# A perceiver layer with experts: the last gathered rows added behind the last pair's hidden products, and one summing operation moved between engines

## The chip, the core and the metric

The kernel runs on one core of a Trainium2 chip. The core has TensorE (PE, matrix products), VectorE (DVE), ScalarE (ACT), GpSimd (POOL) and SyncE (SP, which issues transfers). The metric is the device time of one execution in microseconds; the median of three executions before the change is 1019.1 us (1018.79 to 1021.12).

## What is computed

One layer on 256 tokens of width 512, all in fp32: cross attention (16 query heads, 4 key/value heads of 128, keys from 4096 context rows ahead of the 256 own ones, causal among the own), then a state-space mixer, then a mixture of 32 experts of which every token uses 6. Each part is added to x.

```python
x = x + _L0_xattn_ref(_layernorm(x), ctx_2048, wq, wk, wv, wo, wk_ctx, wv_ctx, ...)
x = x + _L0_attn_ref(_layernorm(x), W_in, conv_w, ..., W_out)      # state-space mixer
x = x + _L0_ffn_ref(_layernorm(x), gate_w, wg, wu, wd, sg, su, sd)
# attention
probs = softmax(q @ k_full.T * scale + mask); out = probs @ v_full
# experts
topk_w, topk_i = top_k(sigmoid(x @ gate_w), 6); topk_w = topk_w / sum(topk_w)
act = silu(x @ wg[e]) * (x @ wu[e])
routed = sum over e of combine[t, e] * (act @ wd[e])
return routed + silu(x @ sg) * (x @ su) @ sd
```

## The kernel before

The 256 tokens are two tiles of 128 (t = 0, 1), the 16 heads four groups g of four. A Python program traces the instructions, and a scheduler of the tile framework then fixes the order of each engine's queue from its own estimate of when things are ready. So the order in a queue is mostly that of the text but not always; `tc.issue_after(ins)` pins what is traced in its block behind `ins` on the same engine (an order, not a wait for the end of `ins`). Tiles come from rings: `pp` has four buffers for exponentials, `ps_sc` three and `ps_o` two banks of PSUM.

**Attention.** It runs in steps s = 0 to 8. Step 0 takes the 256 own keys, steps 1 to 8 take 512 context keys each. `scores` (L554) makes one score block, 128 keys by 512 (four heads times 128 queries), on PE (L559), its exponential on ACT (L562), in step 0 the causal mask of a diagonal block on DVE (L565), and the sum of exponentials in `lacc` on DVE: a copy for the first block of a tile (L568), an add for every other one (L570). `values` (L573) multiplies the exponential with v (L579) two scores later and moves the finished product to `oacc` (L583, L585). A tile's step 0 for one g has one score for t = 0 (its diagonal) and two for t = 1 (the second one diagonal): twelve scores in the order g, t. `lacc` and `oacc` serve before that as room for the queries' rotation (L423 to L426).

Each context step's keys and values are computed by PE beside the attention of the step before, by `fast_steps` (L338): a 2 by 2 block scheme with seven products (p1, p6, p2, p7, p5, p4, p3 in this order) instead of eight. It needs sums of weight blocks. T1, T2, T4 are made early on GpSimd (L323). T3 = b22 - b12 overwrites b12, a block of 128x1024 of the loaded weights `wkv`; GpSimd makes it (L336) behind the last query block's scaling (L450), and p7 is the first to read it. The four sums S1 to S4 of the context's blocks (L348 to L351) are GpSimd's too.

**Experts.** The 32 experts are 16 pairs n (L1321). `gate_up` (L1222) makes one pair's hidden product: PE into `ps_egu`, ACT's silu into `si` (L1231), DVE's product into `hid` (L1233, L1234). For pairs 0 to 12, `down` writes each expert's rows to a memory array `ye`, and each token later gathers its rows from there: `gather` (L1181) is six indirect transfers issued by GpSimd for one token tile (L1187), `add` (L1192) six operations on DVE that add a gathered row times its weight to x (L1194). The last three pairs (13, 14, 15) go another way: `spread_hidden` (L1244) multiplies `hid` with a matrix that puts the experts' rows in token order (PE into `hid_sp` and `rest_sp`, ACT copy at L1252, two DVE copies at L1257, giving `hidS`), and `down_into` (L1259) multiplies by the down weights and accumulates all three pairs in two PSUM banks `total[0]`, `total[1]`, one for each token tile (L1264, three products of 128x512 each, two records apiece in the trace). At the end `finish` (L1354) adds `total` to x on DVE and `store` writes it out.

In the text, round n = 14 reads gate_up(14), add of tile 0, gather of tile 1, turn(15), down_into(13), spread(14); round n = 15 reads gate_up(15), add of tile 1, down_into(14), spread(15); then comes down_into(15).

Of the kernel before, what the change touches and what calls it, by code (L numbers as in the profile page):

```python
# [19 lines left out]
P = 128  # L20
# [26 lines left out]
NE = 32  # L47
# [20 lines left out]
def perceiver_layer(ctx: ExitStack, tc: tile.TileContext, a: dict, out: bass.AP):  # L68
# [65 lines left out]
    def layer(ctx, bounded):  # L134
# [193 lines left out]
        def fast_weights(sums):  # L328
            fw = [wpool.tile([P, KD, 512], FP, tag="w", name=f"fast{i}") for i in range(3)]
            fast["T1"], fast["T2"] = carve(fw[0], T, T)  # L330
            fast["T4"], fast["S1"], fast["S2"] = carve(fw[1], T, (2, 2, P), (2, 2, P))
            fast["S3"], fast["S4"], fast["u3"], fast["u2"] = carve(fw[2], (2, 2, P), (2, 2, P), (2, 256), (2, 256))
            for n, t in zip(("T1", "T2", "T4"), sums):
                S.copy(fast[n], t)
            with tc.issue_after(heads_done[-1]):
                G.tensor_tensor(b12, b22, b12, ALU.subtract)  # L336

        def fast_steps(c, behind=None):  # L338
            ct = ctx_tiles.pop(c)
# [203 lines left out]
        def bounded_attention(beside):  # L543

            pp = pool("pp", 4)
            bq = small.tile([P, 3], FP, tag="bq", name="bq", bufs=1)
            V.tensor_reduce(bq[:, 0:1], qw_bc, AX.X, ALU.max, apply_absolute_value=True)
            V.tensor_reduce(bq[:, 1:2], kw_bc, AX.X, ALU.max, apply_absolute_value=True)
            shift = bq[:, 2:3]
            V.tensor_scalar(shift, bq[:, 0:1], bq[:, 1:2], -float(np.sqrt(HD)), ALU.mult, ALU.mult)  # L550
            V.tensor_scalar(shift, shift, BOUND, None, ALU.add)
            outs = {}

            def scores(s, g, t, n):  # L554

                kT, _, r = kv[s]
                i = keys_of(s, t)[n]
                sc = ps_sc.tile([P, REP * P], FP, tag="sc", name="scT")
                TE.matmul(sc, kT[:, g, i * P:(i + 1) * P], qT[:, t, heads4(g), :].rearrange("p h q -> p (h q)"),  # L559
                          start=True, stop=True)  # L560
                pr = pp.tile([P, REP * P], FP, tag="pr", name="prT")
                S.activation(pr, sc, AF.Exp, bias=shift, scale=SCALE if r is None else r[:, i, g:g + 1])  # L562
                if s == 0 and i == t:
                    p3 = pr.rearrange("p (h q) -> p h q", q=P)
                    V.tensor_tensor(p3, p3, upper.unsqueeze(1).to_broadcast([P, REP, P]), ALU.mult)  # L565
                la = lacc[:, t, g, :]
                if s == 0 and n == 0:
                    V.tensor_copy(la, pr)  # L568
                else:
                    V.tensor_tensor(la, la, pr, ALU.add)  # L570
                return pr

            def values(s, g, t, n, pr):  # L573
                _, v, _ = kv[s]
                keys = keys_of(s, t)
                i, last = keys[n], n == len(keys) - 1
                if n == 0:
                    outs[g, t] = ps_o.tile([P, REP * P], FP, tag="o", name="oT")
                TE.matmul(outs[g, t], v[:, i, g * HD:(g + 1) * HD], pr, start=(n == 0), stop=last)  # L579
                if last:  # L580
                    ov = oacc[:, t, g, :]
                    if s == 0:
                        V.tensor_copy(ov, outs.pop((g, t)))  # L583
                    else:
                        V.tensor_tensor(ov, outs.pop((g, t)), ov, ALU.add)  # L585
                    if s == NC:
                        ps = ps_sc.tile([P, REP * P], FP, tag="sc", name="ps_l")
                        TE.matmul(ps, ones, lacc[:, t, g, :], start=True, stop=True)
                        rl = lacc[:, t, g, :]
                        V.reciprocal(rl, ps)  # L590
                        V.tensor_tensor(aT[:, t, heads4(g), :].rearrange("p h q -> p (h q)"), ov, rl, ALU.mult)

            pending = []
            for s in range(NC + 1):
                if s < NC:
                    steps = [(s, g, t, i) for g in range(NKV) for t in range(NT) for i in range(len(keys_of(s, t)))]
                else:
                    steps = [(s, g, t, i) for t in range(NT) for g in range(NKV) for i in range(len(keys_of(s, t)))]
                    last_weights()
                extra = []  # L600
                if 0 < s < NC:
                    if s + 1 < NC:
                        load_ctx(s + 1)
                    extra = fast_steps(s, heads_done[4] if s == 1 else None)
                    extra.insert(len(extra) // 2, lambda: clear(s - 1))
                done = 0
                for n, st in enumerate(steps):
                    if s == 0 and n == 3:
                        for turn in turns:
                            turn()  # L610
                    pending.append((*st, scores(*st)))
                    if s == 0 and st[3] == len(keys_of(s, st[2])) - 1:
                        q = qT[:, st[2], heads4(st[1]), :]
                        S.activation(q, q, AF.Copy, scale=kw_col)
                    if len(pending) > 2:
                        values(*pending.pop(0))
                    if s < NC:

                        while done < min(len(extra), len(extra) * (n + 1) // (len(steps) - 4)):
                            extra[done]()  # L620
                            done += 1
                    elif n > len(steps) // NT + 1:
                        for f in beside():
                            f()
            for p in pending:
                values(*p)

        def general_attention():
            with ExitStack() as gctx:
# [11 lines left out]
                stats = {}  # L641
                for turn in turns:
                    turn()

                for s in range(NC + 1):
                    if 0 < s < NC:
# [542 lines left out]
                got.append(yk)  # L1189
            return got  # L1190

        def add(got, t):  # L1192
            for k, yk in enumerate(got):
                V.scalar_tensor_tensor(x_sb[:, t, :], yk, m["w8"][:, t, k:k + 1], x_sb[:, t, :], ALU.mult, ALU.add)  # L1194

        class Rounds:


            def __init__(self, ctx, weights):
                pool = lambda name, bufs, **kw: ctx.enter_context(tc.tile_pool(name=name, bufs=bufs, **kw))  # L1200
                self.r, self.weights = 0, weights
                self.e2, self.e4 = pool("e2", 2), pool("e4", 4)
                self.ps_x, self.ps_gu = pool("ps_x", 2, space=PSUM), pool("ps_gu", 2, space=PSUM)
                self.ps_t, self.ps_ye = pool("ps_t", 1, space=PSUM), pool("ps_ye", 3, space=PSUM)
                self.rows, self.xgT, self.hid, self.hidT = {}, {}, {}, {}

            def fetch(self, n):
                for i in range(2):
# [13 lines left out]
            def gate_up(self, n):  # L1222

                hid = self.hid[n] = self.e2.tile([P, 2 * FE], FP, tag="hid", name="hid")
                for i in range(2):
# [5 lines left out]
                    S.activation(si, ps[:, 0:FE], AF.Silu)  # L1231
                    c0 = 2 * P + i * REST
                    V.tensor_tensor(hid[:, i * P:(i + 1) * P], si[:, 0:P], ps[:, FE:FE + P], ALU.mult)  # L1233
                    V.tensor_tensor(hid[:, c0:c0 + REST], si[:, P:FE], ps[:, FE + P:], ALU.mult)  # L1234

            def turn_hidden(self, n):
                tp = self.ps_t.tile([P, 3, P], FP, tag="t", name="hidTp")
# [6 lines left out]
            def spread_hidden(self, n, by):  # L1244
# [9 lines left out]
                    TE.matmul(rest[:, i, :], h[:, 2 * P:3 * P], by[i], start=True, stop=True)  # L1254
                for i in range(2):
                    half = slice(i * REST, (i + 1) * REST)
                    V.tensor_copy(hs[half, 2, :], rest[half, i, :])  # L1257

            def down_into(self, n, total, first, last):  # L1259
                wd = self.weights[3 * n + 2].rearrange("p (j n) -> p j n", j=3)  # L1260
                h = self.hidT.pop(n)
                for t in range(NT):
                    for j in range(3):
                        TE.matmul(total[t], h[:, j, t * P:(t + 1) * P], wd[:, j, :],  # L1264
                                  start=(first and j == 0), stop=(last and j == 2))
# [17 lines left out]
        with ExitStack() as rctx:  # L1283
# [33 lines left out]
                        V.tensor_copy(spread[:, h * (TAIL // 2):(h + 1) * (TAIL // 2), t * P:(t + 1) * P], tp)  # L1317

            FIRST, LAST = HEAD // 2, NP - TAIL // 2
            got, r_y, r_x, r_k = None, (main.e4, "y"), (main.e4, "xg"), (yp, "yk")  # L1320
            for n in range(NP):  # L1321
                main.gate_up(n)
# [2 lines left out]
                if n == LAST + 1:  # L1325
                    add(got, 0)
                    got = gather(ye, row_y, 1, r_y, r_x, r_y, r_x, r_x, r_k)
                if n == LAST + 2:
                    add(got, 1)
                if FIRST <= n + 2 < NP:  # L1330
                    main.fetch(n + 2)
                if FIRST <= n + 1 < NP:
# [3 lines left out]
                elif n > LAST:  # L1336
                    if n == LAST + 1:
                        total = [main.ps_ye.tile([P, DM], FP, tag="ye", name="total") for _ in range(NT)]
                    main.down_into(n - 1, total, n - 1 == LAST, False)
                if n > 0:  # L1340
                    load_piece(3 * (n - 1 + NHELD) + 2)
                if n == FIRST + 1:
# [3 lines left out]
                    got = gather(ye, row_y, 0, r_k, r_y, r_k, r_x, r_k, r_y)  # L1346
                if n < LAST:
                    main.turn_hidden(n)
                else:
                    e0 = 2 * n - (NE - TAIL)  # L1350
                    main.spread_hidden(n, [spread[:, e0 + i, :] for i in range(2)])
            main.down_into(NP - 1, total, False, True)

            def finish(t):  # L1354
# [91 lines left out]
```

## Time and profile before

The profiled execution took 1020.27 us; its span, from the first to the last instruction, is 1018.5 us.

| stretch, us | what runs | PE busy, us | granted clock |
|---|---|---|---|
| 0 to 80 | loads, own queries, keys, values | 74.35 | 1.00 |
| 80 to 100 | step 0 of the attention | 16.79 | 1.00 |
| 100 to 700 | context steps, output projection begun | 599.08 | 1.00 |
| 700 to 850 | mixer, routing | 144.17 | 1.00 |
| 850 to 976 | pairs 0 to 12 | 126.00 | 1.00 |
| 976 to 996 | pairs 13, 14, hidden part of 15 | 20.00 | 1.00 |
| 996 to 1013 | down parts of 14 and 15 | 14.24 | 0.90 |

A line of a group or of the timeline reads: start, length, engine, line of the code, operation, out<-in, shapes, count; in brackets the idle time ahead of it and what ended it. A wait reads: who waited for whom, total, how often, longest. A row of a stretch gives its length, then busy time and count for PE, PEld (weight loads), DVE, ACT, POOL, then the granted clock, the share of the transfer engines and GB/s.

### The profile page before, as it was taken

The numbers are of one execution on the slowest core, as the hardware profiler recorded it, in microseconds if no ns is written. First come the engines' busy times: TensorE is split into PE (matmuls) and PEld (weight loads), VectorE is DVE, ScalarE is ACT, GpSimd is POOL, SyncE is SP. The second block draws the span as 40 slices with busy tenths as digits, with TensorE's granted clock in tenths as the row PEclk, the third lists the DMA queues.
The fourth block names the chain that finished last, engine by engine and source line by source line (L and its number), as shares of the span: only waits on it lengthen the run. The fifth ranks groups of instructions, "written<-read, shape, count | busy, mean of one in ns | idle before, by whom it ended". The sixth has DMA issues, their size and how long they took to land.

```text
span 1018.5 us, 9069 instructions
## 1 busy us (share of the span) xinstructions
PE 994.6 (98%) x2786; PEld 477.5 (47%) x2786; DVE 502.3 (49%) x983; ACT 392.0 (38%) x862; POOL 155.8 (15%) x156
## 2 busy tenths in 40 slices
PE   7998999999999999999999999999999999999996
PEld 3443444444444444444444444444656555555553
DVE  4466555454454454453544544575886662312233
ACT  3644544343443443443444434441446421222210
POOL 5343002001101101101200200000141321000031
PEclk9999999999999999999999999999999999999998
DMA  9725045132222313313304203600364368999732
GB/s 338 214 61 164 2 132 209 32 90 80 57 48 97 82 32 113 84 23 122 82 11 134 64 2 81 165 1 0 102 210 156 115 216 321 355 355 369 272 107 84
DMA packets 136557, 131.94 MB, mean 130 GB/s; under 512 B 80402, under 2 KB 99763, under 8 KB 135347
## 3 DMA queue, kind: packets, MB, share of 16 engines
q1 hardware_dynamic: 129392, 115.71, 35.8%
q0 software_dynamic: 2208, 8.39, 2.4%
q10 hardware_dynamic: 4898, 7.16, 1.9%
q8 instruction: 24, 0.39, 0.1%
q14 instruction: 35, 0.28, 0.1%
HBM read 90.86 MB, written 40.39 MB: 129 GB/s over the span
## 4 chain that ended last, share of the span: by engine, by line
PE 91%; DVE 2%; issue 2%; POOL 1%; DMA 1%; ACT 1%; SPq 0%; DVEq 0%; POOLq 0%; ACTq 0%
PE oT L579 22%; PE scT L559 22%; PE ps_kv L356 16%; PE ps_egu L212 8%; PE ps_self L212 3%; PE ps_ye L1273 2%; PE ps_v L212 2%; PE ps_o L771 2%; PE ps_xbc L212 1%; PE ps_ye L1276 1%; PE ps_k L212 1%; PE ps_out L961 1%; PE xgTp L1218 1%; PE total L1264 1%; PE ps_yd L901 1%
## 5 line engine op out<-in xcount | busy, mean ns | idle before, releaser
L570 DVE TENSOR_TENSOR lacc<-lacc,prT 128x512 f32<-128x512 f32 x260 | 185.4, 714 | 240.7 <-ACT prT L562 239.8
L562 ACT ACTIVATE prT<-scT,bq,rk 128x512 f32<-128x512 f32 x256 | 198.9, 777 | 254.6 <-PE scT L559 242.5
L579 PE MATMUL oT<-prT,v 128*128 128x512 f32 x536 | 272.5, 593 | 4.1 <-DVE prT L565 2.8
L559 PE MATMUL scT<-qT,kT 128*128 128x512 f32 x536 | 270.9, 592 | 0.0
L579 PEld LDWEIGHTS oT<-prT,v 128*128 128x128 f32 x536 | 101.3, 190 | 133.9 <-issue 116.7
L559 PEld LDWEIGHTS scT<-qT,kT 128*128 128x128 f32 x536 | 101.2, 190 | 124.6 <-issue 122.4
L190 POOL TENSOR_TENSOR rk<-pv,mhalf 128x4 f32<-128x4 f32 x32 | 32.3, 1010 | 371.0 <-DVE pv L189 371.0
L1233 DVE TENSOR_TENSOR hid<-si,ps_egu 128x128 f32<-128x128 f32 x32 | 9.2, 287 | 94.2 <-ACT si L1231 94.2
L356 PE MATMUL ps_kv<-wkv,fast 128*128 128x512 f32 x112 | 53.4, 592 | 0.0
L248 ACT ACTIVATE sq<-kraw 128x128 f32<-128x128 f32 x128 | 35.6, 278 | 44.9 <-DVE kraw L374 42.8
L356 PE MATMUL ps_kv<-wkv,ctx 128*128 128x512 f32 x112 | 52.8, 592 | 0.0
L356 PE MATMUL ps_kv<-fast,fast 128*128 128x512 f32 x112 | 52.6, 592 | 0.0
L585 DVE TENSOR_TENSOR oacc<-oT,oacc 128x512 f32<-128x512 f32 x64 | 43.7, 683 | 0.0
L1187 POOL DMA_INDIRECT yk<-ye,row_y x12 | 13.3, 1112 | 139.1 <-DVE hid L1234 135.8
L1279 ACT COPY y_sb<-ps_ye 128x512 f32<-128x512 f32 x26 | 15.2, 586 | 48.8 <-PE ps_ye L1276 43.0
L356 PEld LDWEIGHTS ps_kv<-wkv,fast 128*128 128x128 f32 x112 | 21.3, 190 | 26.8 <-issue 26.8
L356 PEld LDWEIGHTS ps_kv<-wkv,ctx 128*128 128x128 f32 x112 | 21.3, 190 | 26.8 <-issue 23.7
L356 PEld LDWEIGHTS ps_kv<-fast,fast 128*128 128x128 f32 x112 | 21.3, 190 | 26.8 <-issue 21.8
L1231 ACT ACTIVATE si<-ps_egu 128x192 f32<-128x192 f32 x32 | 10.6, 332 | 58.5 <-PE ps_egu L212 56.2
L374 DVE TENSOR_TENSOR kraw<-ps_kv,fast 128x256 f32<-128x256 f32 x42 | 17.8, 424 | 27.9 <-PE ps_kv L356 27.9
L771 PE MATMUL ps_o<-wo,qT 128*128 128x512 f32 x64 | 28.8, 592 | 0.0
L212 PE MATMUL ps_self<-wq,xT 128*128 128x512 f32 x64 | 28.1, 592 | 0.0
(294 smaller groups left out, 1120.6 us busy)
## 6 DMA issues: line engine op xcount, KB each, us to landing
xg<-xn SPq DMA_DIRECT2D x6, 2560.0 KB, 9.3
w_in<-in_pairs_dram SPq DMA_DIRECT2D x14, 768.0 KB, 7.0
ctx<-in_ctxT_dram SPq DMA_DIRECT2D x7, 1024.0 KB, 9.3
kd<-tr SPq DMA_DIRECT2D x112, 64.0 KB, 2.0
kT<-kd SPq DMA_DIRECT2D x28, 256.0 KB, 2.8
xg_sb<-xg SPq DMA_DIRECT2D x28, 256.0 KB, 6.2
ye<-y_sb ACTq DMA_DIRECT2D x26, 256.0 KB, 7.1
wkv<-in_pairs_dram SPq DMA_DIRECT2D x6, 768.0 KB, 7.1
```

Source lines behind the costliest of these rows:

```text
L190: return G.tensor_tensor(dst, v[:, :n], mhalf[:, :n], ALU.pow)
L212: TE.matmul(ps, lhs(k), rhs_of(k), start=(k == 0), stop=(k == KD - 1))
L248: S.activation(sq[:, h, :], raw[:, h, :], AF.Square, accum_out=ss[:, h:h + 1])
L356: TE.matmul(ps, lhs(k), rhs(k), start=(start and k == 0), stop=(k == 1), skip_group_check=True)
L374: V.tensor_tensor(to[n], ps[:, n, :], more[:, n, :], ALU.add)
L559: TE.matmul(sc, kT[:, g, i * P:(i + 1) * P], qT[:, t, heads4(g), :].rearrange("p h q -> p (h q)"), start=True, stop=True)
L562: S.activation(pr, sc, AF.Exp, bias=shift, scale=SCALE if r is None else r[:, i, g:g + 1])
L570: V.tensor_tensor(la, la, pr, ALU.add)
L579: TE.matmul(outs[g, t], v[:, i, g * HD:(g + 1) * HD], pr, start=(n == 0), stop=last)
L585: V.tensor_tensor(ov, outs.pop((g, t)), ov, ALU.add)
L771: TE.matmul(m["ps_o", t], aT[:, t, h, :], wo[j][:, h % 4, :], start=(h == 0), stop=(h == NH - 1))
L1273: TE.matmul(ps[i], h[:, i, :], wd[:, i, :], start=True, stop=False)
```

## The change

Three edits.

- Step 0's sums. For t = 0 the exponential is written straight into `lacc` and masked there, with no copy. For t = 1 the first exponential is kept, and one add of both writes `lacc`. The eight copies at L568 go.
- T3 = b22 - b12 is made by VectorE instead of GpSimd, traced ahead of the ninth score and pinned behind the mask of the seventh.
- The last round. The add of tile 1 leaves its place after gate_up(15). down_into(14) is cut in its two token tiles, and between them stand three of the six adds, spread(15) and the other three adds. The first three are pinned behind the last hidden product of pair 15, the second three behind the last DVE copy of spread(15).

The diff, cut to its core (the new order of round 15 is in its last part):

```diff
-            with tc.issue_after(heads_done[-1]):
-                G.tensor_tensor(b12, b22, b12, ALU.subtract)
+        def last_sum():
+            V.tensor_tensor(b12, b22, b12, ALU.subtract)
...
-                pr = pp.tile([P, REP * P], FP, tag="pr", name="prT")
+                la = lacc[:, t, g, :]
+                alone = s == 0 and t == 0
+                pr = la if alone else pp.tile([P, REP * P], FP, tag="pr", name="prT")
                 S.activation(pr, sc, AF.Exp, bias=shift, scale=SCALE if r is None else r[:, i, g:g + 1])
                 if s == 0 and i == t:
                     p3 = pr.rearrange("p (h q) -> p h q", q=P)
-                    V.tensor_tensor(p3, p3, upper.unsqueeze(1).to_broadcast([P, REP, P]), ALU.mult)
-                la = lacc[:, t, g, :]
-                if s == 0 and n == 0:
-                    V.tensor_copy(la, pr)
+                    masked.append(V.tensor_tensor(p3, p3, upper.unsqueeze(1).to_broadcast([P, REP, P]), ALU.mult).ins)
+                if s == 0:
+                    if n < t:
+                        first_pr.append(pr)
+                    elif not alone:
+                        V.tensor_tensor(la, first_pr.pop(), pr, ALU.add)
                 else:
                     V.tensor_tensor(la, la, pr, ALU.add)
...
+                    if s == 0 and n == 8:
+                        with tc.issue_after(masked[-1]):
+                            last_sum()
...
-        def add(got, t):
-            for k, yk in enumerate(got):
+        def add(got, t, ks=range(TOPK)):
+            for k in ks:
+                yk = got[k]
                 V.scalar_tensor_tensor(x_sb[:, t, :], yk, m["w8"][:, t, k:k + 1], x_sb[:, t, :], ALU.mult, ALU.add)
...
-                    V.tensor_tensor(hid[:, c0:c0 + REST], si[:, P:FE], ps[:, FE + P:], ALU.mult)
+                    self.done[n] = V.tensor_tensor(hid[:, c0:c0 + REST], si[:, P:FE], ps[:, FE + P:], ALU.mult).ins
...
-                    V.tensor_copy(hs[half, 2, :], rest[half, i, :])
+                    self.done[n] = V.tensor_copy(hs[half, 2, :], rest[half, i, :]).ins
...
-            def down_into(self, n, total, first, last):
+            def down_into(self, n, total, first, last, tiles=range(NT)):
...
-                if n == LAST + 2:
-                    add(got, 1)
...
-                    main.down_into(n - 1, total, n - 1 == LAST, False)
+                    if n == NP - 1:
+                        main.down_into(n - 1, total, False, False, [0])
+                        with tc.issue_after(main.done[n]):
+                            add(got, 1, range(0, TOPK // 2))
+                        spread_last(n)
+                        with tc.issue_after(main.done[n]):
+                            add(got, 1, range(TOPK // 2, TOPK))
+                        main.down_into(n - 1, total, False, False, [1])
+                    else:
+                        main.down_into(n - 1, total, n - 1 == LAST, False)
```

Here NP is 16, LAST is 13, and `spread_last(n)` calls `spread_hidden` as the loop did before. The branch for unbounded scores, which isn't taken, calls `last_sum` too.

More of the change, by code (lines that the diff above doesn't have):

```diff
@@ L551, in bounded_attention @@
             V.tensor_scalar(shift, shift, BOUND, None, ALU.add)
-            outs = {}
+            outs, first_pr, masked = {}, [], []
             def scores(s, g, t, n):
@@ L643, in general_attention @@
                     turn()
+                last_sum()
                 for s in range(NC + 1):
@@ L1204, in __init__ @@
                 self.ps_t, self.ps_ye = pool("ps_t", 1, space=PSUM), pool("ps_ye", 3, space=PSUM)
-                self.rows, self.xgT, self.hid, self.hidT = {}, {}, {}, {}
+                self.rows, self.xgT, self.hid, self.hidT, self.done = {}, {}, {}, {}, {}
             def fetch(self, n):
@@ L1256, in spread_hidden @@
                     half = slice(i * REST, (i + 1) * REST)
-                    V.tensor_copy(hs[half, 2, :], rest[half, i, :])
-            def down_into(self, n, total, first, last):
+                    self.done[n] = V.tensor_copy(hs[half, 2, :], rest[half, i, :]).ins
+            def down_into(self, n, total, first, last, tiles=range(NT)):
                 wd = self.weights[3 * n + 2].rearrange("p (j n) -> p j n", j=3)
-                h = self.hidT.pop(n)
-                for t in range(NT):
+                h = self.hidT[n]
+                for t in tiles:
                     for j in range(3):
@@ L1319, in layer, with spread_last @@
             FIRST, LAST = HEAD // 2, NP - TAIL // 2
+            def spread_last(n):
+                e0 = 2 * n - (NE - TAIL)
+                main.spread_hidden(n, [spread[:, e0 + i, :] for i in range(2)])
             got, r_y, r_x, r_k = None, (main.e4, "y"), (main.e4, "xg"), (yp, "yk")
@@ L1348, in layer @@
                     main.turn_hidden(n)
-                else:
-                    e0 = 2 * n - (NE - TAIL)
-                    main.spread_hidden(n, [spread[:, e0 + i, :] for i in range(2)])
+                elif n < NP - 1:
+                    spread_last(n)
             main.down_into(NP - 1, total, False, True)
```

## The prediction

> **What bounds the kernel now.** I read the page's busy times first, then the waits of TensorE (PE), then busy time by stretch, then the timeline of the two stretches where PE is not busy.
>
> ```profile
> PE 994.6 (98%) x2786; PEld 477.5 (47%) x2786; DVE 502.3 (49%) x983; ACT 392.0 (38%) x862; POOL 155.8 (15%) x156
> ...
> PEclk9999999999999999999999999999999999999998
> ```
>
> PE is busy 994.6 of 1018.5 us, so a change that adds or removes no matmul can win only out of the 23.9 us in which PE stands still, and out of the one slice (the last) whose granted clock is below 9 tenths. The waits of PE, with total, count and longest, say which of them the change can touch:
>
> ```profile
> PE oT L579 <- DVE prT L565: 2.8, 2, 1.6
> PE total L1264 <- DVE hidS L1257: 2.6, 1, 2.6
> PE oT L579 <- ACT prT L562: 0.9, 1, 0.9
> PE oT L579 <- DVE oacc L583: 0.4, 1, 0.4
> ```
>
> The stretches, with each engine's busy time and the granted clock:
>
> ```profile
> 80.00:100.00 20.00, 16.79 (x40) 6.63 (x39) 13.26 (x17) 8.76 (x15) 7.64 (x5) 1.00 0.53 159
> 100.00:700.00 600.00, 599.08 (x1397) 264.99 (x1396) 303.57 (x492) 251.50 (x519) 58.69 (x53) 1.00 0.26 75
> ...
> 996.00:1013.00 17.00, 14.24 (x33) 6.32 (x31) 6.89 (x15) 0.92 (x2) 2.58 (x3) 0.90 0.24 76
> ```
>
> Attention is a full PE from 100 to 700 us: what is won before 100 is kept, since PE has nothing to wait for afterwards. PE idles 3.2 us in 80 to 100 and 2.8 us in 996 to 1013, where the clock is also down. Both are places of the diff.
>
> **First step (80 to 100 us).** Number the twelve scores of step 0 as s0 to s11, their value products v0 to v11.
>
> ```profile
> 81.48 0.93 DVE L565 TENSOR_TENSOR prT<-prT,upper 128x512 f32<-128x512 f32 x1 [1.82 <-ACT prT L562]
> 81.82 2.80 POOL L336 TENSOR_TENSOR wkv<-wkv 128x1024 f32<-128x1024 f32 x1
> 82.45 2.46 DVE L568 COPY lacc<-prT 128x512 f32<-128x512 f32 x1
> ...
> 85.46 1.13 DVE L565 TENSOR_TENSOR prT<-prT,upper 128x512 f32<-128x512 f32 x1
> 86.01 1.71 POOL L351 TENSOR_TENSOR fast<-ctx,fast 128x512 f32<-128x512 f32 x1
> 86.51 1.48 DVE L568 COPY lacc<-prT 128x512 f32<-128x512 f32 x1
> ...
> 89.85 1.12 PE L579 MATMUL oT<-prT,v 128*128 128x512 f32 x2 [1.22 <-DVE prT L565]
> ```
>
> A copy at L568 takes 0.43 us alone (its median), yet these two take 2.46 and 1.48 us and end with the GpSimd sums beside them (L336 ends at 84.62, L351 at 87.72). The mask of s3 therefore starts only at 89.12, though its exp ended at 85.6, and v3 waits for it.
>
> Removed: eight copies at L568 (four for query tile 0, whose exp now writes lacc itself; four for tile 1, whose first add takes two tiles). At 0.43 us that is 3.4 us of DVE, as drawn in this trace more, 2.0 + 1.05 us for the two stretched ones. Removed from GpSimd: L336, 2.80 us; its two sums behind it (L350, L351, 1.46 + 1.71 us) move up to about 81.9 to 85.0. Added on DVE: the same subtraction, 128x1024. From rows of two SBUF inputs (0.41 us for 256 columns, 0.69 for 512) I estimate 1.24 us. It is queued behind the mask of s6 (98.40 to 99.09 before), so behind it stand the copy of oT (L583) and the mask of s8. There DVE idled 0.76 and 0.94 us between 99.1 and 102.7 and loses a 0.43 us copy at either end; I take 0. Without that cover it costs 1.24 us once, on v8. Its reader, the product with T3, ran at 122.4, 20 us later.
>
> New DVE line: mask s0 to 82.4, transpose 0.70, mask s2 1.13 (a GpSimd sum still beside it) to 84.3, oT copy 0.68, add 0.69, mask s3 to 86.3. PE line at 0.86 us for each product of two records: v0 82.4, selfT 83.3, s3 83.8, v1, s4, v2 at 86.3, s5 87.2, v3 88.05 (mask ready), v4 88.9, v5 at 89.8 (s5's exp ends about 88.95, its mask 89.7), end 90.6. Before, v5 ended at about 93.06. **Gain 2.4 us.** What comes late next is v6: s6 runs behind two filler products, ended at 97.43, and v6 started at 99.14, waiting for exp (0.69) and mask (0.69). Nothing in the diff shortens this 1.7 us; it moves with the rest.
>
> The rule that speaks against this part stands in the Trainium skill, GPSIMD Engine Reference, section 1 "Specifications": the SBUF interface is shared with VectorE, and not only copies in a two-port mode contend, but also operations with two SBUF inputs. The masks and adds that stay are of that kind, and the two sums now meet them earlier. By the rule alone each of some three such operations could stretch as a copy does (1.0 to 2.0 us), and the gain would be nought. By the row, a mask beside L351 took 1.13 instead of 0.69 us: plus 0.44. I take the row, since it is the same operation beside the same sum; bounds of the head: gain 0 to 4 us (the latter if v6's wait also goes).
>
> **Last pair (976 to the end).** The order on DVE decides here:
>
> ```profile
> 998.93 0.75 DVE L1194 SCALAR_TENSOR_TENSOR x_sb<-yk,lacc,x_sb 128x512 f32<-128x512 f32 x1 [0.57 <-DMA yk<-ye,row_y]
> 999.60 0.85 DVE L1257 COPY hidS<-rest_sp 64x256 f32<-64x256 f32 x2
> ...
> 1001.82 0.75 DVE L1194 SCALAR_TENSOR_TENSOR x_sb<-yk,lacc,x_sb 128x512 f32<-128x512 f32 x1 [0.59 <-DMA yk<-ye,row_y]
> 1002.60 0.29 DVE L1233 TENSOR_TENSOR hid<-si,ps_egu 128x128 f32<-128x128 f32 x1
> ```
> ```profile
> 1002.00:1005.30 3.30, 3.30 (x6) 1.24 (x5) 1.31 (x5) 0.00 (x0) 0.00 (x0) 0.50 0.01 2
> ```
>
> rest_sp of pair 14 was ready at about 991, its copies ran at 999.60 behind ten adds, each waiting for its gathered row; PE stood 2.62 us (997.88 to 1000.50). Pair 15's hid products ran at 1002.60 though the first si was ready at 994.0. After that the clock fell to 0.50 for about 3.4 us (half of it, 1.7 us, lost), and 0.25 us went on pair 15's hidS (L1252, ended 1007.39). Together 4.6 us.
>
> In the change the second tile's six adds stand behind pair 15's hid products, three before and three behind pair 15's hidS copies. The twelve GpSimd gathers stay in place and order (982.48 to 999.2); no queue is moved past, since the SP and ACT queues have no transfer left there but the stores. The gather buffers are held longer, but no later fetch wants them. DVE then: the first tile's last add ends 995.2 (its row's arrival); pair 14's two copies, 0.86, to 996.1; hid products to 997.1 (second si at 996.58); adds 7 to 9, rows there by 997.61, to 999.2; pair 15's copies when rest_sp is done; adds 10 to 12, last row at 1001.82, to 1003.5. PE at 0.43 us a record of 512 columns and 0.215 of 256 (12 in 5.15 us, 4 in 0.86 before): from 996.00 six records of total 0 to 998.57 (pair 14's copies are there at 996.1, needed at 997.7), spread of pair 15, eight records, to 1000.3 (hid there at 997.1), six records of total 1 to 1002.9, which hide hidS (rest copies 1000.5 to 1001.4), twelve of pair 15 to 1008.0. Before, the last record ended at 1012.7. **Gain 4.6 us** (4.7 less 0.1 for waits on semaphores). The adds cost nothing while PE's twelve last records cover them; uncovered, three cost 2.1 us. The stores follow the last product as before.
>
> Here a second rule speaks against: TensorE: Matmul & The Clock Gate, Part 1, gives a window of about 3.4 us of idling before the clock halves, and warns of gaps above some 3 us. This gap is 2.62 us, so read strictly the halving is not the gap's and would stay: gain 2.9. The row says the halving came 1.4 us after that gap and lasted 3.4 us, and that other gaps of 1.7 us left 1.00. I take the row: no gap, no halving.
>
> **Sum.** The profiled execution took 1020.27 us, 1018.5 of span and 1.8 around it. 1020.3 - 2.4 - 4.6 = 1013.3; that execution lies 1.2 above the median of 1019.1, so the median should be 1012.1.
>
> **Rivals.**
> - Both gains as summed: 1012.1. Chance 0.60.
> - The scheduler, planning with a lighter DVE, also puts something between s6 and v6: up to 1.7 us more, 1010.4. For it: q's transpose at 84.83 comes up to 2.4 us sooner and its heads with it. Against: the filler order is set by q's transfer, which is not edited. 0.12.
> - The head gives nothing (masks stretched by the two sums, or PE merely waits longer for v6): 1014.5. 0.14.
> - The tail gives 2.9 (clock halves anyway, or pair 14's copies are queued behind pair 15's hid products): 1013.8. 0.06.
> - Slower: the order of each queue is the scheduler's, not the text's (two products of step 1 ran before s6), and an edit at 80 us makes it plan anew all that follows. If each of the seven context steps got one exposed exp and mask of 1.7 us like v6's, 12 us are lost: 1024. It decides from 1.0 us a step (7.0 in all). Against it: two scores stand between a score and its value product throughout, and PE lost 0.9 us in 600. 0.04.
> - The adds are pulled ahead in another form, or the edges do nothing: about 1017. 0.04.
>
> About 0.3% (3.1 us) is what a measurement of this kernel can tell from no change. Faster by more: 0.91; within: 0.05; slower: 0.04. The range from 1010.0 to 1014.8 leaves out the last two cases and parts of the second and third.
>
> **What would show it.** Right: no wait of total on L1257 and a last slice of PEclk at 9; the last matmul's end about 7 us sooner; no row of L336 or of copies into lacc in step 0; PE's wait for masks before the first ps_kv gone, v6's 1.5 still there. Wrong: a wait of hid_sp on hid, or of total on hidS or yk; a clock of 0.5 without a gap; PE idle between 100 and 700 us.

## The result, and the profile after

The changed kernel took 1013.84 us (median of 5 executions, 1013.70 to 1014.24), the kernel before beside it 1021.08 (1018.79 to 1021.29). The ratio is 0.9938, with a 95% interval of 0.9923 to 0.9952, so about 6.3 us are saved. The profiled execution took 1013.77 us, its span is 1012.0. The kernel before scatters by 2.5 us from one execution to the next, the changed one by 0.5; why is part of the answer below. Two executions of the kernel before on a third chip, of 1517 and 4641 us, are left out of everything that follows.

The page of the changed kernel, its busy times and clock:

```profile
span 1012.0 us, 9057 instructions
...
PE 992.4 (98%) x2786; PEld 477.8 (47%) x2786; DVE 498.6 (49%) x976; ACT 391.7 (39%) x862; POOL 152.6 (15%) x155
...
PEclk9999999999999999999999999999999999999999
```

The number of PE's instructions is the same, its busy time is 2.2 us less although no product was removed: 1.7 us of that is the stretch at half clock, gone from the last slice. ("Half clock" is a granted clock of 0.50 in the rows.) The longest waits of PE:

```profile
PE ps_k L212 <- DMA wkv<-in_wk_ctx_dram: 5.5, 1, 5.5
PE oT L586 <- DVE lacc L570: 1.5, 1, 1.5
PE ps_sh L1064 <- DVE sh L1059: 0.9, 1, 0.9
```

The wait of `total` on the hidS copies is not in the list any more, and of the waits on masks only the one that the prediction left (v6) remains. Busy time by stretch, columns as before:

```profile
80.00:100.00 20.00, 18.47 (x49) 8.02 (x47) 10.49 (x16) 9.93 (x16) 5.41 (x4) 1.00 0.64 199
...
100.00:700.00 600.00, 599.08 (x1397) 265.07 (x1396) 301.88 (x488) 250.66 (x518) 58.66 (x53) 1.00 0.26 74
```

Step 0 on the timeline of the changed kernel (GpSimd's last scaling and its two sums, VectorE's masks and adds, PE's value products):

```profile
81.30 1.04 POOL L452 TENSOR_TENSOR lacc<-lacc,r 128x512 f32<-128x512 f32 x1
82.02 0.87 DVE L570 TENSOR_TENSOR lacc<-lacc,upper 128x512 f32<-128x512 f32 x1 [1.88 <-ACT lacc L567]
82.30 1.73 POOL L352 TENSOR_TENSOR fast<-ctx 128x512 f32<-128x512 f32 x1
...
83.79 0.79 DVE L570 TENSOR_TENSOR prT<-prT,upper 128x512 f32<-128x512 f32 x1 [0.28 <-ACT prT L567]
83.99 1.72 POOL L353 TENSOR_TENSOR fast<-ctx,fast 128x512 f32<-128x512 f32 x1
...
85.10 1.16 DVE L575 TENSOR_TENSOR lacc<-prT 128x512 f32<-128x512 f32 x1
86.18 0.68 DVE L570 TENSOR_TENSOR lacc<-lacc,upper 128x512 f32<-128x512 f32 x1
...
88.64 1.02 PE L586 MATMUL oT<-lacc,v 128*128 128x512 f32 x2
...
97.09 1.22 DVE L338 TENSOR_TENSOR wkv<-wkv 128x1024 f32<-128x1024 f32 x1
97.23 1.12 PE L586 MATMUL oT<-lacc,v 128*128 128x512 f32 x2 [1.51 <-DVE lacc L570]
```

The mask of s3 (86.18) is done long before v3 (88.64), which has no wait in brackets. The subtraction sits behind the mask of s6, takes 1.22 us, and v6 starts beside it. From the first transpose of step 0 on PE (selfT, 79.26 before, 79.75 now) to the second product of context step 1 (117.27 and 115.36) it was 38.01 us and is now 35.61: **2.40 us** saved. The last round on VectorE:

```profile
991.22 0.75 DVE L1206 SCALAR_TENSOR_TENSOR x_sb<-yk,lacc,x_sb 128x512 f32<-128x512 f32 x1 [0.64 <-DMA yk<-ye,row_y]
991.89 0.85 DVE L1269 COPY hidS<-rest_sp 64x256 f32<-64x256 f32 x2
992.77 0.29 DVE L1245 TENSOR_TENSOR hid<-si,ps_egu 128x128 f32<-128x128 f32 x1
...
995.04 2.32 DVE L1206 SCALAR_TENSOR_TENSOR x_sb<-yk,lacc,x_sb 128x512 f32<-128x512 f32 x3
998.60 0.86 DVE L1269 COPY hidS<-rest_sp 64x256 f32<-64x256 f32 x2 [1.24 <-PE rest_sp L1266]
999.48 2.33 DVE L1206 SCALAR_TENSOR_TENSOR x_sb<-yk,lacc,x_sb 128x512 f32<-128x512 f32 x3
```

Each three adds now run in one piece: their rows have come by then, and no add stands ahead of something PE wants. PE has no gap here: six records of `total` at 994.09, the spread at 996.67, six at 998.39, twelve at 1000.97. From pair 13's first `total` product (983.97 before, 982.05 now) to the end of the span it was 34.53 us and is 29.95: **4.6 us** saved in these two executions.

### The profile page after: what moved, and what is told of

It is laid out like the page before. It is cut to its first block, busy times and chain, and to the rows that moved or that the text cites. A ratio compares the mean times of both kernels' runs of the same rounds, so it can differ in the third digit from the quotient of the medians.

```text
span 1012.0 us, 9057 instructions
## 1 busy us (share of the span) xinstructions
PE 992.4 (98%) x2786; PEld 477.8 (47%) x2786; DVE 498.6 (49%) x976; ACT 391.7 (39%) x862; POOL 152.6 (15%) x155
## 4 chain that ended last, share of the span: by engine, by line
PE 95%; DVE 1%; ACT 1%; POOL 1%; DMA 1%; issue 0%; SPq 0%; ACTq 0%
PE oT L586 23%; PE scT L561 23%; PE ps_kv L358 17%; PE ps_egu L212 8%; PE ps_self L212 3%; PE ps_ye L1285 2%; PE ps_v L212 2%; PE ps_o L782 2%; PE total L1276 2%; PE ps_xbc L212 1%; PE ps_ye L1288 1%; PE ps_k L212 1%; PE xgTp L1230 1%; PE ps_out L972 1%; PE ps_yd L912 1%; DMA wkv<-in_wk_ctx_dram 1%
## 5 line engine op out<-in xcount | busy, mean ns | idle before, releaser
L577 DVE TENSOR_TENSOR lacc<-lacc,prT 128x512 f32<-128x512 f32 x256 | 182.7, 715 | 240.5 <-ACT prT L567 239.7
L586 PE MATMUL oT<-prT,v 128*128 128x512 f32 x528 | 268.0, 592 | 0.9 <-ACT prT L567 0.9
```

## Experiments

Each kernel's executions stand beside those of the kernel before on the same chip. "Head" is the time on PE from the first selfT of step 0 to the second product of context step 1 (38.01 us before, 35.61 in the change), "tail" the time from pair 13's first `total` product to the end of the span (34.53 and 29.95), both from the profiled execution.

**The kernel before, again** (no edit).

> The kernel before, unchanged, to see what its own runs spread by: they lay at 1018.8 to 1019.1 and at 1021.1 to 1021.3. Theory A (the clock's halving behind PE's 2.6 us gap falls or does not fall in a run, 1.7 us each time): a mean granted clock of 0.997 goes with the long runs and 0.999 with the short ones, some 2 us apart. Theory B (the spread is in the loads at the start or around the span): clock the same in all runs, times still some 2 us apart.

Measured: 1020.06 us, ratio 0.9996 (0.9984 to 1.0008). Head 38.01, tail 35.4. With the 31 executions of the kernel before that ran beside it there are 45. The 16 with a mean granted clock of 0.999 or more have a median of 1019.08 us (1018.18 to 1020.04), the 12 with 0.997 or less one of 1021.6 (1020.64 to 1022.87). The other 17 have 0.998 and lie between 1017.93 and 1022.79: their mean doesn't tell the two cases apart, because it also counts half clock behind the last product, where it costs nothing (2.9 us in the profile of the kernel before, from 1015.58 on). So theory A holds for the two outer groups, which don't overlap on any of the three chips used; there they lie 2.5, 2.3 and 2.0 us apart. The half clock costs 1.7 of that; the rest is not explained. The profiled execution of this run shows the stretch:

```profile
1002.00:1003.00 1.00, 1.00 (x3) 0.48 (x2) 0.21 (x2) 0.00 (x0) 0.00 (x0) 0.50 0.04 16
1003.00:1004.00 1.00, 1.00 (x2) 0.38 (x2) 0.97 (x4) 0.00 (x0) 0.00 (x0) 0.50 0.00 0
```

The clock records of the traces say more. In all twelve profiled executions the full clock begins 8.6 to 14.5 us into the span, and from there every change of it falls on a multiple of 3.413 us, to three digits (291 of them before the half clock of the kernel before, 289 to 291 in the other profiles that show it). So the span can be cut at these times, a different set in each execution. In the kernel before:

```profile
998.51:1001.92 3.41, 1.42 (x4) 0.70 (x5) 2.35 (x5) 0.00 (x0) 0.68 (x1) 1.00 0.50 149
1001.92:1005.33 3.41, 3.41 (x6) 1.35 (x5) 1.39 (x5) 0.00 (x0) 0.00 (x0) 0.50 0.01 2
1012.17:1015.58 3.41, 0.69 (x2) 0.00 (x0) 0.69 (x1) 0.00 (x0) 0.00 (x0) 1.00 0.38 138
1015.58:1018.50 2.92, 0.00 (x0) 0.00 (x0) 0.00 (x0) 0.00 (x0) 0.00 (x0) 0.50 0.05 14
```

and at the end of this run:

```profile
1012.10:1015.52 3.42, 1.58 (x4) 0.38 (x2) 0.69 (x1) 0.00 (x0) 0.00 (x0) 1.00 0.29 108
1015.52:1018.93 3.41, 0.00 (x0) 0.00 (x0) 0.00 (x0) 0.00 (x0) 0.00 (x0) 1.00 0.20 65
```

A piece in which PE idled 1.99 us (3.41 less 1.42) was followed by half clock, one with 1.83 us was not. In all twelve profiles, every piece at full clock with 1.99 us or more was followed by half clock and none with 1.83 or less was. So not the gap's length alone decides, but how much of it falls into one piece. By these figures a gap of 2.62 us, cut in the middle, should cost no clock (an estimate); all six profiled gaps of 2.2 to 3.1 us happened to lie the other way.

**Only the last round of the change**, step 0 as before.

```diff
-                    if n < t:
-                        first_pr.append(pr)
-                    elif not alone:
-                        V.tensor_tensor(la, first_pr.pop(), pr, ALU.add)
+                if s == 0 and n == 0:
+                    V.tensor_copy(la, pr)
...
+            with tc.issue_after(heads_done[-1]):
+                G.tensor_tensor(b12, b22, b12, ALU.subtract)
```

> Only the last round of the change, step 0 and the GpSimd subtraction as before. Theory (the two gains are apart and add up): 4.6 us below the kernel before, no wait of total on the hidS copies, clock 0.999, PE's waits on masks in 80 to 100 us as before (2.8 us). Rival (the clock halves anyway, it is not the gap's): 2.9 us.

Measured: 1016.15 us (1015.88 to 1016.62), ratio 0.9959 (0.9944 to 0.9975), some 4.2 us. Head 38.01, tail 29.96, no half clock. Against the kernel before's executions of high mean clock it is 2.9 us shorter, against those of low clock 5.5. So the rival's figure is met where nothing had been halved before, but not its reason: the half clock went with the gap. Where the clock had been halved, more is saved than the theory's 4.6.

**Only step 0 of the change**, the last round as before.

```diff
+                if n == LAST + 2:
+                    add(got, 1)
...
-                        main.down_into(n - 1, total, False, False, [0])
-                        with tc.issue_after(main.done[n]):
-                            add(got, 1, range(0, TOPK // 2))
...
+                    main.down_into(n - 1, total, n - 1 == LAST, False)
```

> Only step 0's sums and the moved subtraction, last round as before. Theory: 2.4 us below the kernel before, the tail's wait of 2.6 us on the hidS copies back, and with it a clock of about 0.5 for some 3.4 us in at least a part of the runs. Rival (the head's gain is an accident of the load at the start, 0.5 us there): 0 to 1 us.

Measured: 1017.33 us (1015.62 to 1020.07), ratio 0.9972 (0.9963 to 0.9982), 2.9 us (1.8 to 3.8). Head 35.61, to the hundredth that of the change; tail 35.1 with the gap and the half clock back:

```profile
PE total L1276 <- DVE hidS L1269: 3.1, 1, 3.1
```
```profile
1000.00:1001.00 1.00, 1.00 (x2) 0.34 (x1) 0.97 (x4) 0.00 (x0) 0.00 (x0) 0.50 0.00 0
```

The two gains are apart and add up: the last round alone took 1016.15, less step 0's 2.40 this makes 1013.75, and the change took 1013.84. The rival (an accident of the first loads) falls.

**The change without the cut of pair 14's down product.**

```diff
-                        main.down_into(n - 1, total, False, False, [0])
+                        main.down_into(n - 1, total, False, False)
...
-                        main.down_into(n - 1, total, False, False, [1])
```

> The whole change, but pair 14's down product is not cut: both token tiles, then three adds, spread of pair 15, three adds. Theory (what counts is the order on VectorE, hidS copies and hid products ahead of the adds; the cut only hides pair 15's hidS): within 0.3 us of the change, PE waiting 0.3 us at most on pair 15's hidS. Rival (the cut is what carries the tail): 1 us or more slower than the change.

Measured: 1013.84 us (1013.50 to 1014.07), ratio 0.9937 (0.9921 to 0.9952), the same as the change. Tail 30.15, 0.2 more. Putting the spread of pair 15 between the two halves thus hides 0.2 us in the profile and nothing that the medians show; the order on VectorE is what counts.

**Step 0's copies alone** (subtraction on GpSimd, last round as before).

```diff
-        def last_sum():
-            V.tensor_tensor(b12, b22, b12, ALU.subtract)
+            with tc.issue_after(heads_done[-1]):
+                G.tensor_tensor(b12, b22, b12, ALU.subtract)
```

> Head, first half alone: no copies in step 0, the subtraction stays on GpSimd, last round as before. Theory (the copies are held until the GpSimd sum beside them ends, operations with two inputs are only slowed): most of the head's 2.4 us, 1.9 us below the kernel before; masks and adds beside the sums 0.9 to 1.2 us. Rival by the skill's wording (two-input operations contend just as copies do): under 0.8 us, masks beside the 2.8 us subtraction stretched to 2 us and more.

Measured: 1018.14 us (1015.45 to 1021.08), ratio 0.998 (0.997 to 0.9989). Head 36.11, so 1.90 saved. But masks beside the subtraction and the sums took far longer than the theory said:

```profile
84.36 2.81 POOL L336 TENSOR_TENSOR wkv<-wkv 128x1024 f32<-128x1024 f32 x1
...
85.85 1.88 DVE L568 TENSOR_TENSOR prT<-prT,upper 128x512 f32<-128x512 f32 x1 [0.27 <-ACT prT L565]
...
87.13 1.73 POOL L350 TENSOR_TENSOR fast<-ctx 128x512 f32<-128x512 f32 x1
...
87.65 0.68 DVE L588 COPY oacc<-oT 128x512 f32<-128x512 f32 x1
88.25 1.16 DVE L573 TENSOR_TENSOR lacc<-prT 128x512 f32<-128x512 f32 x1
...
88.83 1.71 POOL L351 TENSOR_TENSOR fast<-ctx,fast 128x512 f32<-128x512 f32 x1
...
89.33 1.75 DVE L568 TENSOR_TENSOR lacc<-lacc,upper 128x512 f32<-128x512 f32 x1
```

GpSimd's three operations ran from 84.36 to 90.54 in this execution, and each of the three long operations of VectorE ends 0.54 to 0.56 us behind the end of the GpSimd operation that it began beside (87.73 behind 87.17, 89.41 behind 88.86, 91.08 behind 90.54). In the kernel before, the mask of 85.46, which took 1.13 us and ended at 86.59, had begun beside this one, which ended at 86.04:

```profile
84.58 1.46 POOL L350 TENSOR_TENSOR fast<-ctx 128x512 f32<-128x512 f32 x1
```

So masks and adds are held as the copies are; how long depends on how much of the GpSimd operation is left. The theory's "only slowed" is wrong, and so is the rival's 0.8 us, though the rival has the mechanism. The copy out of PSUM among them (L588) kept its 0.68 us. PE paid about 0.45 us at the second long mask (v3 starts 9.34 us behind the first selfT, 8.89 in the change); there was slack for the rest.

**The moved subtraction alone** (copies as before, last round as before).

```diff
-                pr = la if alone else pp.tile([P, REP * P], FP, tag="pr", name="prT")
+                pr = pp.tile([P, REP * P], FP, tag="pr", name="prT")
...
+                if s == 0 and n == 0:
+                    V.tensor_copy(la, pr)
```

> Head, second half alone: the subtraction on VectorE, the eight copies stay, last round as before. Theory: the copies still meet the two remaining GpSimd sums, now some 2.8 us earlier; one copy stretched to about 1.2 us, 1.5 us below the kernel before. Then the two halves do not add up (1.9 + 1.5 against 2.4). Rival (the subtraction alone is the cause): the full 2.4 us.

Measured: 1017.96 us (1015.12 to 1019.21), ratio 0.9975 (0.9966 to 0.9985). Head 35.85, so 2.16 saved, more than the 1.5 expected. One copy is stretched, to 1.38 us, near what was expected, but the next one is not:

```profile
82.83 1.38 DVE L570 COPY lacc<-prT 128x512 f32<-128x512 f32 x1
84.12 0.70 DVE L254 STREAM_TRANSPOSE tr<-lacc 128x512 f32<-128x512 f32 x1
84.75 1.13 DVE L568 TENSOR_TENSOR prT<-prT,upper 128x512 f32<-128x512 f32 x1
85.81 0.41 DVE L570 COPY lacc<-prT 128x512 f32<-128x512 f32 x1
```

Either half alone saves most of the head, 1.90 and 2.16 of 2.40: both shorten the same queue of VectorE ahead of the mask of s3, and once that mask is early enough PE has no more to gain. Counted from the first selfT, that mask ends at 10.54 us before, at 9.28 and 8.38 with either half, and at 7.11 with both, while PE, with nothing to wait for, gets to v3 at 8.89.

**The change without the pins.**

```diff
-                        with tc.issue_after(main.done[n]):
-                            add(got, 1, range(0, TOPK // 2))
+                        add(got, 1, range(0, TOPK // 2))
                         spread_last(n)
-                        with tc.issue_after(main.done[n]):
-                            add(got, 1, range(TOPK // 2, TOPK))
+                        add(got, 1, range(TOPK // 2, TOPK))
```

> The whole change, but without the two pins: the adds of tile 1 stand in the new place of the text and nothing orders them behind pair 15's hid products. Theory (the order on VectorE is the whole gain; left alone the scheduler puts the adds ahead again, and the cut then hurts, since half of the down product no longer covers the late hid products): PE waits twice, about 2.5 us on pair 14's hidS and 2.3 us on pair 15's hid, 5 to 6 us slower than the change with the clock's halving. Rival (the place in the text is enough): as the change.

Measured: 1020.91 us (1020.07 to 1022.43), ratio to the kernel before 1.0009 (1.0002 to 1.0017): 7.1 us more than the change, so none of the gain is left. Step 0's is still there (head 35.62), but the last round is 2.7 us longer than in the kernel before (tail 37.2). In all its 22 executions the mean clock was 0.997 or less. PE's waits:

```profile
PE total L1276 <- DVE hidS L1269: 2.8, 1, 2.8
...
PE hid_sp L1262 <- DVE hid L1245: 1.4, 1, 1.4
```
```profile
1000.00:1003.00 3.00, 2.00 (x5) 1.64 (x6) 1.37 (x5) 0.00 (x0) 0.00 (x0) 0.50 0.01 3
1003.00:1006.00 3.00, 3.00 (x7) 1.89 (x6) 0.84 (x2) 0.59 (x1) 0.00 (x0) 0.51 0.02 5
```

The scheduler did put the adds ahead again. The second wait is shorter than expected and the half clock longer, two pieces of 3.413 us (999.13 to 1005.96; PE idled 1.38 us within the first and the clock stayed at 0.50); the 7.1 us lie above the 5 to 6 expected. With the cut, the new place in the text without the pins is thus worse than the old one; without the cut it was not run.

**The change with one product moved on PE**, to take away v6's wait. A variant of the change, run twice.

```diff
-                TE.matmul(sc, kT[:, g, i * P:(i + 1) * P], qT[:, t, heads4(g), :].rearrange("p h q -> p (h q)"),
-                          start=True, stop=True)
+                made.append(TE.matmul(sc, kT[:, g, i * P:(i + 1) * P], qT[:, t, heads4(g), :].rearrange("p h q -> p (h q)"),
+                                      start=True, stop=True).ins)
...
                 def p1():
                     m["x"] = bank()
-                    product(m["x"], here(j, 0), w11)
+                    with tc.issue_after(score) if score and j == 1 else nullcontext():
+                        product(m["x"], here(j, 0), w11)
```

In context step 1 `score` is `made[6]`, the product of s6; in the others there is none.

> The whole change, and the first product of context step 1 pinned on PE behind the seventh score of step 0, so that it lies between that score and its value product. Theory (PE's remaining 1.5 us there is the exposed exp and mask, and PE never waits again until 700 us): 1.5 us faster than the change, that wait gone. Rival (the score was late because its queries arrive late): the wait turns up ahead of the score, no gain.

Measured: 1011.90 us (1011.56 to 1014.04), ratio to the kernel before 0.9928 (0.9905 to 0.995). Two of the six took 1014.04 and 1013.94, the first of them profiled, with the late start that is told at the end. The second time it ran on one chip with the change itself:

> The change, unchanged, beside the next kernel on one chip. Theory (without the gap at the end no run has a mean clock of 0.997 or less): runs within 0.5 us of each other near 1013.8, but for runs whose first products come 2 us late as in the profile of the score-first kernel.

> The change with the first product of step 1 behind the seventh score, again, for a comparison on one chip. Theory: 1.7 us below the change (its value product waits no more, and the step of 1.7 us in the stretch from selfT to p2 is kept to the end). Rival (lost again later): less than 0.5 us.

Measured: the change 1013.77 us (1013.32 to 1014.02), this version 1011.88 (1011.65 to 1012.86), ratios to the kernel before 0.9939 (0.9923 to 0.9954) and 0.9923 (0.9907 to 0.9938). The change's six spread by 0.70 us instead of the expected 0.5. Each of this version's six is shorter than each of the change's, and the medians are 1.9 us apart. Head 33.89 in the first profile, 1.72 less than the change. PE in the second:

```profile
90.95 1.02 PE L562 MATMUL scT<-qT,kT 128*128 128x512 f32 x2
91.81 1.88 PE L358 MATMUL ps_kv<-wkv,ctx 128*128 128x512 f32 x4
93.52 1.08 PE L587 MATMUL oT<-lacc,v 128*128 128x512 f32 x2
94.44 1.88 PE L358 MATMUL ps_kv<-fast,fast 128*128 128x512 f32 x4
```

s6 runs at 90.95, right after v5; its exp and mask lie beside p1, and v6 follows with no wait. The queries had been there; the scheduler had only put s6 behind both fillers. This beats both kernels.

## Why the prediction was right, and where it was off

- **Step 0 gains 2.4 us**: measured 2.40, alone (head of "only step 0") and in the change. The queue on VectorE came in the forecast order. Its two stretched operations, the mask of s2 and the add, were forecast at 1.13 and 0.69 us and took 0.79 and 1.16: the sum came out near, the split did not.
- **The subtraction on VectorE, 1.24 us, hidden**: 1.22 us, and no wait on it. Only the copy of oT stood behind it.
- **What stays beside the GpSimd sums (row against rule)**: here the prediction was right by luck. It took the 0.44 us that one mask had lost for the price of meeting a sum, but that price isn't fixed. In step 0 of all twelve profiles, each operation of 128x512 with two SBUF inputs that ran on beyond its 0.69 us ended 0.54 to 0.56 us behind the end of a GpSimd operation. The prediction's own mask, put down to L351, ended at 86.59 and had met the last 0.6 us of L350 (which ended at 86.04). In the change these operations took 0.79, 0.87 and 1.16 us, since they began late in a GpSimd operation; beside the longer subtraction, 1.88. So the rule of the Trainium skill (GPSIMD Engine Reference, section 1 "Specifications"), that operations with two inputs contend too, was the better guide. What was wrong in the reading of it was to let each of three such operations lose 1.0 to 2.0 us; with the subtraction gone from GpSimd, little was left for them to wait for.
- **v6's wait stays**: 1.51 us in the change. Taking it away shortened the head by 1.72 us and the median by 1.9. No transfer held it.
- **Last round, PE's line**: forecast from the first of pair 14's `total` products to the end of the last record 12.0 us (996.0 to 1008.0), measured 12.2 (994.09 to 1006.28). Forecast gain 4.6, tail measured 4.6 in the two profiled executions.
- **No gap, no half clock (row against rule)**: right. In 35 executions of the four kernels that keep the new, pinned order no mean clock lay below 0.998, and their six profiles show half clock only behind the last product. The kernel before had 35 of 113 at 0.997 or less on three chips, and the version without pins 22 of 22. The profiled executions with gaps of 2.2 to 3.1 us all show the half clock. The 3.4 us of idling that the Trainium skill gives (TensorE: Matmul & The Clock Gate, Part 1) is longer than any of these gaps: here pieces of 3.41 us that were idle for 1.99 us were enough. Its remark that the window runs freely agrees with the multiples of 3.413 us, which begin at another time in each execution. That this is why a part of the executions is spared follows from them but is not shown, as no profiled gap was spared.
- **The cut hides hidS**: right, and it is worth 0.2 us at most.
- **The step that was off**: "that execution lies 1.2 above the median of 1019.1, so the median should be 1012.1". The sum for the profiled execution was 1013.3, and it took 1013.77; the remaining 0.5 us are the later start of step 0 (79.75 for 79.26). But the 1.2 us between the profiled execution and the median were not a constant around the span. The profiled execution had a half clock in its last round, and the tail's gain of 4.6 us counts 1.7 us for it. The median of three, 1019.1, was most likely an execution without: its clock is not on record, but of the 45 on one chip none with 0.997 or less lay below 1020.64, and those with 0.999 or more have the median 1019.08. The change takes that difference away: its profiled execution and its median are 0.07 us apart. So the 1.2 us were taken off twice, and the median came out at 1013.84 instead of 1012.1. Three executions were too few besides: over all 113 the median is 1020.49, and the profiled execution with its 1020.27 was an ordinary one.
- **What was luck**: the saving beside it, 6.3 us, lies near the forecast 7.0 because the kernel before came out on both sides there. Against its executions of whole clock on the chip of the run above (1019.08) the change saves 5.2 us, against the halved ones (1021.6) 7.8.
- **The rivals**: "the tail gives 2.9" named the measured median, 1013.8, and for an execution with the clock whole 2.9 us is what the tail gives; its reasons (the clock halves anyway, the copies are queued late) didn't come true. The gain that comes with a new plan of the scheduler did not come by itself (the order of s6 and v6 is the old one); the head did not vanish; no context step lost anything (599.08 us busy of 600, as before).

## What to carry to other kernels

An operation that waits for a transfer should not stand in an in-order queue ahead of one that the busiest engine wants: look at what is queued behind each wait, and pin the order, since the place in the text is not the place in the queue. Price a gap of the matrix engine with the half clock behind it, and check in several executions how often that happens, before one profiled execution is converted to a median. Two edits that shorten the same queue do not add up (1.90 and 2.16 gave 2.40), so test each alone before keeping both.

## What the runs showed of the hardware

- A gap of 2.2 us on PE was enough for a granted clock of 0.50 over 3.41 us; gaps of 1.5 to 1.6 us in step 0 left it at 1.00 in every profiled execution that had them. The clock changed only at multiples of 3.413 us, and what counted at full clock was the idle time within one such piece: 1.99 us halved the next, 1.83 did not.
- A copy of 128x512 fp32 in SBUF beside a GpSimd operation took 1.38 to 2.46 us instead of 0.43 and ended 0.27 to 0.29 us behind it; masks and adds with two SBUF inputs took up to 1.88 instead of 0.69 and ended 0.54 to 0.56 us behind it; a copy out of PSUM kept its 0.68.
- A second scatter of about 2 us, seen in two profiled executions (copies alone, and the first of the score-first version): twenty records of the first key product take 11.3 us instead of 9.0 to 9.2, and step 0 starts at 81.7 to 81.8 instead of 79.3 to 79.9. In both, two records a microsecond are done from 10 to 13 us and three or four from 14 us on, and the trace's first clock record, full clock, begins at 14.4 and 14.5 us; in the other ten it begins at 8.6 to 11.1. The first four records take 3.3 to 3.8 us everywhere, about half the later pace. So PE starts at half pace and gets to the full one later in these two; the clock row reads 1.00 there only because nothing is recorded before. Why it came later is open.
